# Self attention in a perceiver block: 128-wide weight transposes, values by head parity, weighing over four quarters of the array

## The chip, the cores and the metric

One NeuronCore of a Trainium2 chip runs the whole kernel. The metric is the device time of one execution in microseconds, as the median of several runs. A profile of one execution comes with it: a page of summary views, and a trace of every instruction with its start, its duration and what it waited for. TensorE is called PE in these views, its weight loads PEld, VectorE DVE, ScalarE ACT, GpSimd POOL, and SyncE, which issues the DMAs, SP.

## What is computed

Sixteen sequences of 64 rows of 512 pass through three residual blocks: a cross attention to a context of 512 rows, a self attention with two softmaxes a head, and a feed-forward with 4-bit rounding of its operands. The change touches the second block and the hand-over to the third. The second, cut to what matters:

```
x = x + self_attention(layernorm(x))
q, k, v = z @ Wq.T, z @ Wk.T, z @ Wv.T        # 8 heads, in q and k two halves of 32 a head
q, k = rope(q), rope(k)
o1 = softmax(q1 @ k1.T * d**-0.25) @ v        # v: 64 wide a head
o2 = softmax(q2 @ k2.T * d**-0.25) @ v
o = o1 - lam * o2
o = o * rsqrt(mean(o*o) + eps) * ln_w + ln_b  # over a head's 64
return (o * (1 - LAMBDA_INIT)) @ Wo.T
```

The feed-forward is `silu(gate) * up`, then `down`, where each operand is rounded in blocks of 16 (a block's maximum, a scale, a rounding, the scale again).

## The kernel before

Rows are taken in eight tiles of 128, each two sequences (e = 0, 1) of 64 rows. Matmuls that need precision are split: an operand is a high part (`copy` to the rounded type on ScalarE) and a low part (the difference, on VectorE or POOL), and a product of 128x512 is twelve matmuls in three groups of four (`terms`, L114). Plain fp32 matmuls stand as two records each in the profile; transposes as one.

`cross_attention` (L346) ends with the start of the self attention: the weights Wq, Wk, Wv, Wo are loaded and split (`split`, L1146), and tiles 0 and 1 get their first products. Then `SelfAttention.rest` (L1369) runs a software pipeline over the tiles n = 2 to 7. A round n does for tile n the products Wq, Wk, Wv, rope (`rope`, L1183: VectorE multiplies by the tables at L1198 and L1200, POOL adds at L1206), the transposes of q and k (`turn_qk`, L1209: qt and kt on TensorE, copies qT and kT on ScalarE at L1216), the scores (`scores`, L1219: sc), and the softmax (`softmax`, L1236: mx at L1245 and ex at L1246 on VectorE; exp at L1255; the sum at L1260). In the same round tile n-1 gets the mix of its two softmaxes (`mix`, L1265: VectorE at L1268, POOL at L1271), the transpose of the mixed weights w (`turn_w`, L1275: wt on TensorE at L1282, the copy wT at L1290), the weighing of the values (`weigh`, L1292: o at L1298), the squares (L1308) and the norm's factor (`rms`, L1310; two POOL operations, rstd). Tile n-2 gets `scale` (L1316, VectorE), `turn_o` (L1320: ot, then oT at L1326 and a split) and `out` (L1338: the product wo and the addition of x, VectorE, L1346). Tile n+1 gets its norm z (ScalarE, L166) and its transpose zt with the split into zh and zl (`turn`, L1161). `end` (L1348) holds the order from qt to the sum.

The order of each engine is the order in which the program writes it: `in_order` (L82), called at the end of `rest`, ties every instruction so far to the one before it on its engine. The feed-forward's later steps are placed by a scheduler, which also draws some of their layer-norm statistics (st_f, mv_f) forward into the gaps of `rest`.

Into the rounds 3 to 7 are laid the norm steps of the feed-forward's tiles 0 and 1: `norm_steps` (L1492) gives seven steps a tile (statistics; normalise; then the five steps of `fp4_steps`, L180: maxima and scales at L194 to L197; POOL's multiplication L199; a VectorE operation L202 with a Relu on ScalarE L205; two VectorE operations L207 and L208; POOL's multiplication L210). `rest` says in `parts` how many steps go ahead of `out`, behind it, and behind `end`.

```python
norms = iter(first[:3] + second[:1] + first[3:4] + second[1:2] + first[4:] + second[2:])
parts = {3: (1, 0, 1), 4: (2, 1, 1), 5: (1, 1, 1), 6: (1, 1, 0), 7: (1, 1, 1)}
```

PSUM has eight banks of 128x512. Three turn round for products and transposes (`mm` and `tr`, L99 and L102: the same three), two pairs turn round for scores and gate/up products (`two`, L105), one is for weighing and for down products (`ps_av`). A tile waits for the last reader of the one whose place it takes.

After the rounds the written order goes on: the gate and up products of (tile 0, chunk 0), the rest of tiles 6 and 7, first steps of the feed-forward (`gate` L1521, `gated` L1534, `quantise`). Loads of the feed-forward's weights (`weights`, L1451) are issued from SP at fixed places of this order.

Of the kernel before, what the change touches and what calls it, by code (L numbers as in the profile page):

```python
# [9 lines left out]
F32 = mybir.dt.float32  # L10
# [3 lines left out]
AF = mybir.ActivationFunctionType  # L14
ALU = mybir.AluOpType
# [4 lines left out]
P = 128  # L20
D = 512
KC = D // P
B = 16
S = 64
N = 512
NJ = N // P
NT = B * S // P
FF = 1408
BLK = 16
CHUNKS = [(at, min(D, FF - at)) for at in range(0, FF, D)]  # L30
# [15 lines left out]
def f32(t):  # L46

    return t.bitcast(F32)


class Common:
# [75 lines left out]
    def split(self, hi, lo, src, by=None):  # L127

        self.nc.scalar.copy(hi, src)  # L129
        (by or self.nc.vector).tensor_tensor(lo, src, f32(hi), ALU.subtract)  # L130
# [165 lines left out]
class Context:  # L296
# [59 lines left out]
    def high(self, b, c):  # L356
        if b < B:
            if c == 0:
                self.done[b] = tuple(
                    self.cm.slot(6 + 2 * (b % 2) + h, f"x{h}_{b}") for h in range(2)  # L360
                )
            self.cm.nc.scalar.copy(self.done[b][0][:, c, :], self.raw[:, c, :])  # L362

    def low(self, b, c):
        if b < B:
            hi, lo = (t[:, c, :] for t in self.done[b])
            by = (self.cm.nc.vector, self.cm.nc.gpsimd)[c % 2]
            by.tensor_tensor(lo, self.raw[:, c, :], f32(hi), ALU.subtract)  # L368
# [360 lines left out]
def cross_attention(tc, cm, sc, i, cw, cx, w1, w2, att, quant):  # L729

    nc = tc.nc
# [9 lines left out]
    for e in range(2):  # L741
        t = w2.tile([P, S + N + S + KC * S], F32, tag=f"fx{e}", name=f"mask{e}")
# [202 lines left out]
    def out_product(p):  # L945
        oh, ol = state.pop(("oT", p))
        po = cm.mm(f"po_{p}")
        cm.product(
            po, lambda k: (oh[:, k, :], ol[:, k, :], w_o[0][:, k, :], w_o[1][:, k, :]), range(KC)
        )  # L950
        state["po", p] = po, cm.moments(po, f"o_{p}")

    def out_norm(p):
        po, mv = state.pop(("po", p))
        z = w2.tile([P, D], F32, tag="one", name=f"oz_{p}")
        cm.normalize(z, po, f"o_{p}", mv)
        state["oz", p] = z

    def out_add(p):
        z = state.pop(("oz", p))  # L960
        nc.gpsimd.tensor_tensor(z, z, rows_o["g_o"], ALU.mult)
        nc.gpsimd.tensor_tensor(z, z, rows_o["b_o"], ALU.add)
        nc.gpsimd.tensor_tensor(cm.x[p], cm.x[p], z, ALU.add)

    def out_moments(p):
        cm.shift(cm.x[p], f"a_{p}", cm.x_mv[:, p, :])
# [140 lines left out]
    att.values(0)  # L1107
    out_moments(NT - 2)
    att.end(0, sum=False)
    att.split("Wo", 0, 1)  # L1110
    att.sum(0)
    att.product(1, "Wq")
    att.mix(0)
# [4 lines left out]
    att.rope(1, "Wk")  # L1118
    att.norm(2)
    out_product(NT - 1)  # L1120
    att.split("Wo", 2, 3)
    out_norm(NT - 1)
    att.end(1)
    assert not quant.active and not quant.jobs
    return {2: lambda: out_add(NT - 1), 3: lambda: out_moments(NT - 1)}


class SelfAttention:
# [15 lines left out]
        self.nc.sync.dma_start(raw, self.i[name].rearrange("(k p) n -> p k n", p=P))  # L1144

    def split(self, name, *ks):  # L1146
        cm, raw = self.cm, self.st[name, "raw"]
        if ks[0] == 0:
            at = self.HOME[name]
            self.W[name] = cm.slot(at, f"{name}h"), cm.slot(at + 1, f"{name}l")  # L1150
        hi, lo = self.W[name]
        for k in ks:
            cm.split(hi[:, k, :], lo[:, k, :], raw[:, k, :], (self.nc.vector, self.nc.gpsimd)[k % 2])

    def norm(self, t):
        cm = self.cm
# [20 lines left out]
        self.st["ps", t, name] = ps  # L1177

    def values(self, t):
        v = self.st["v", t] = self.w1.tile([P, D], F32, tag="v", bufs=4, name=f"v_{t}")  # L1180
        self.nc.scalar.copy(v, self.st.pop(("ps", t, "Wv")))

    def rope(self, t, name):  # L1183
        nc, w1, sa = self.nc, self.w1, self.sa
# [90 lines left out]
    def turn_w(self, t):  # L1275
        cm, nc = self.cm, self.nc
        w = self.st.pop(("w", t))
        pt = cm.tr(f"wt_{t}").rearrange("p (h n) -> p h n", n=S)
        for h in range(8):
            for e in range(2):  # L1280
                rows = slice(e * S, (e + 1) * S)
                nc.tensor.matmul(  # L1282
                    pt[rows, h, :],
                    lhsT=w[rows, h, :],
                    rhs=cm.ident[rows, rows],
                    start=True,
                    stop=True,
                )
        wT = self.st["wT", t] = self.w2.tile([P, 8, S], F32, tag="four0", name=f"wT_{t}")
        nc.scalar.copy(wT, pt)  # L1290

    def weigh(self, t):  # L1292
        v, wT = self.st.pop(("v", t)), self.st.pop(("wT", t))
        po = self.st["po", t] = self.cm.ps_av.tile([P, 8, S], F32, tag="av", name=f"o_{t}")
        for h in range(8):
            for e in range(2):
                rows = slice(e * S, (e + 1) * S)
                self.nc.tensor.matmul(  # L1298
                    po[rows, h, :],
                    lhsT=wT[rows, h, :],  # L1300
                    rhs=v[rows, h * S : (h + 1) * S],
                    start=True,
                    stop=True,
                )

    def squares(self, t):
        o = self.st["o", t] = self.w1.tile([P, 8, S], F32, tag="oh", name=f"on_{t}")
        self.nc.scalar.activation(o, self.st["po", t], AF.Square)  # L1308

    def rms(self, t):  # L1310
        cm = self.cm
# [3 lines left out]

    def scale(self, t):  # L1316
        r = self.st.pop(("r", t)).unsqueeze(2).to_broadcast([P, 8, S])
        self.nc.vector.tensor_tensor(self.st["o", t], self.st.pop(("po", t)), r, ALU.mult)

    def turn_o(self, t):  # L1320
        cm, nc, sa = self.cm, self.nc, self.sa
# [16 lines left out]
    def out(self, t):  # L1338
        cm = self.cm
        oh, ol = self.st.pop(("oT", t))  # L1340
        ps = cm.mm(f"wo_{t}")
        wh, wl = self.W["Wo"]
        cm.product(
            ps, lambda k: (oh[:, k, :], ol[:, k, :], wh[:, k, :], wl[:, k, :]), range(KC)
        )
        self.nc.vector.tensor_tensor(cm.x[t], ps, cm.x[t], ALU.add)  # L1346
# [22 lines left out]
    def rest(self, ff, last):  # L1369

        first, second = (ff.norm_steps(t) for t in range(2))
        norms = iter(first[:3] + second[:1] + first[3:4] + second[1:2] + first[4:] + second[2:])


        parts = {3: (1, 0, 1), 4: (2, 1, 1), 5: (1, 1, 1), 6: (1, 1, 0), 7: (1, 1, 1)}

        def steps(n, part):  # L1380
            for _ in range(parts[n][part] if n in parts else 0):
                next(norms)()

        for n in range(2, NT):
            self.product(n, "Wq")
            self.scale(n - 2)
            self.product(n, "Wk")
            if n == NT - 1:
                ff.weights(("g", 1))
            self.mix(n - 1)  # L1390
            self.turn_o(n - 2)
            self.rope(n, "Wq")
            self.product(n, "Wv")
            if n == NT - 1:
                ff.weights(("u", 1), ("d", 0))
            self.values(n)
            if n + 1 < NT:
                self.norm(n + 1)
            self.rope(n, "Wk")
            steps(n, 0)  # L1400
            if n == NT - 1:
                ff.turn(0)
            self.out(n - 2)
            last.get(n, lambda: None)()
            if n == 2:
                ff.weights(("g", 0), ("u", 0))
            steps(n, 1)
            self.end(n)
            steps(n, 2)
        assert not list(norms)  # L1410
        ff.gate((0, 0))
        self.scale(NT - 2)
        self.mix(NT - 1)
        ff.up((0, 0))
        self.turn_o(NT - 2)
        ff.gated((0, 0))
        ff.turn(1)
        ff.gate((0, 1))
        self.turn_w(NT - 1)
        ff.quantise((0, 0))  # L1420
        ff.weights(("d", 1))
        ff.gate((1, 0))
        self.weigh(NT - 1)
        self.squares(NT - 1)
        self.rms(NT - 1)
        self.out(NT - 2)
        ff.weights(("g", 2))
        ff.up((0, 1))
        self.scale(NT - 1)
        ff.hidden((0, 1))  # L1430
        self.turn_o(NT - 1)
        ff.up((1, 0))
        ff.hidden((1, 0))
        ff.turn_h((0, 0))
        self.out(NT - 1)
        ff.weights(("u", 2), ("d", 2))
        self.cm.in_order()


class FeedForward:  # L1440
# [65 lines left out]

    def turn(self, t):
        cm, w2 = self.cm, self.w2
        pt = cm.tr(f"xt_{t}")
        cm.transpose_chunks(pt, self.st.pop(("z", t)), KC)  # L1510
        both = w2.tile([P, 2, KC, P], F32R, tag=f"fx{t % 2}", name=f"fx_{t}")
        cm.split(both[:, 0], both[:, 1], pt.rearrange("p (k n) -> p k n", n=P))
        self.st["x", t] = both[:, 0], both[:, 1]
# [6 lines left out]

    def gate(self, s):  # L1521
        t, c = s
        both = self.cm.two(f"gu_{t}_{c}")
        self.st["gu", s] = [both[:, w, : CHUNKS[c][1]] for w in range(2)]
        self.half(s, "g", self.st["gu", s][0])

    def up(self, s):
# [177 lines left out]
```

## Time and profile before

| | |
|---|---|
| median of 3 runs | 918.56 us (917.95 to 920.64) |
| the profiled execution | 917.56 us, span 915.8 us |
| TensorE's granted clock | 0.999 of full speed |
| TensorE busy, 600 to 617 us and 652 to 669 us | 16.42 and 16.67 of 17 us |
| VectorE busy, the same stretches | 12.19 and 12.53 us |
| TensorE busy, 750 to 916 us | 161.30 of 166 us |

The busy shares of the stages come from the view of engine time by stretch. In a line of the timeline the columns are: start and duration in us, engine, line of the kernel, operation, the tile written and the tiles read, partitions and elements, count, and in brackets the engine's idle time ahead of it with what ended it. A line of the waits gives the waiting engine and line, what it waited for, the sum in us, how often, and the longest.

### The profile page before, as it was taken

To read this page: it belongs to the slowest core of one execution; us is meant where nothing else is said; L and a number is where in the kernel's file an instruction comes from. 1 tells how busy PE (TensorE), PEld (TensorE's weight loads), DVE (VectorE), ACT (ScalarE), POOL (GpSimd) and SP (SyncE) were. 2 spreads that over 40 slices of the span, in tenths; PEclk is the share of its full clock that TensorE was granted. 3 is DMA by queue.
4 is the path that set the end of the run, shared out by engine and by line. 5 is a ranking of instruction groups with operands and counts; after the bars stand their busy time and mean duration, and the time that the engine had idled before them with its cause. 6 is when DMAs were issued, how large, how long until landed. Compare 5 with 4: busy or idle time off the path is not lost.

```text
span 915.8 us, 17531 instructions
## 1 busy us (share of the span) xinstructions
PE 896.2 (98%) x6774; PEld 741.3 (81%) x6774; DVE 687.8 (75%) x1386; ACT 392.7 (43%) x750; POOL 330.0 (36%) x376
## 2 busy tenths in 40 slices
PE   5999999999999999999999999999999999999998
PEld 5898777878887788787878887878778788888886
DVE  6544467788799787786987864576887698888875
ACT  4464444444454434444544455434444333322221
POOL 5245153335253353252533522565564320100000
PEclk9999999999999999999999999999999999999999
DMA  7464565544465445445644351140005530000000
GB/s 246 169 242 138 160 185 159 175 157 145 152 184 155 140 143 166 128 131 143 198 135 149 104 168 70 48 184 3 1 1 232 207 138 12 13 12 12 13 12 23
DMA packets 80234, 111.11 MB, mean 121 GB/s; under 512 B 33160, under 2 KB 38808, under 8 KB 78872
## 3 DMA queue, kind: packets, MB, share of 16 engines
q1 hardware_dynamic: 79992, 109.48, 37.2%
q8 instruction: 53, 0.87, 0.4%
q0 software_dynamic: 160, 0.52, 0.2%
q14 instruction: 29, 0.24, 0.1%
HBM read 84.26 MB, written 25.72 MB: 120 GB/s over the span
## 4 chain that ended last, share of the span: by engine, by line
PE 86%; DVE 6%; DMA 2%; ACT 2%; POOL 1%; SPq 1%; issue 1%; ACTq 0%; DVEq 0%; POOLq 0%
PE pk L121 19%; PE pv L121 18%; PE gu L121 13%; PE dn L121 7%; PE av L904 4%; PE sim L836 4%; PE prt L171 3%; PE lv L121 2%; PE po L121 2%; PE lq L121 2%; PE lk L121 2%; PE wo L121 2%; PE Wv L121 2%; PE ht L171 1%; DMA raw_wo<-in_w_out_dram 1%; PE Wq L121 1%
## 5 line engine op out<-in xcount | busy, mean ns | idle before, releaser
L121 PE MATMUL pv<-xvh,x 128*128 128x512 f32 x512 | 133.1, 392 | 0.0
L121 PE MATMUL pk<-x,xkh 128*128 128x512 f32 x512 | 130.4, 397 | 0.0
L121 PEld LDWEIGHTS pk<-x,xkh 128*128 128x128 f32 x512 | 93.7, 188 | 25.4 <-issue 3.9
L121 PEld LDWEIGHTS pv<-xvh,x 128*128 128x128 f32 x512 | 95.3, 188 | 23.3 <-issue 2.2
L810 DVE TENSOR_TENSOR k<-pk,row 128x512 f32<-128x512 f32 x64 | 43.7, 684 | 47.4 <-PE pk L121 47.4
L823 ACT ACTIVATE v<-pv,rs 128x512 f32<-128x512 f32 x64 | 43.9, 686 | 79.2 <-PE pv L121 79.1
L859 ACT ACTIVATE pr<-pr,least 128x576 f32<-128x576 f32 x64 | 49.2, 772 | 55.3 <-DVE least L855 55.0
L368 POOL TENSOR_TENSOR x<-raw,x 128x512 fp32r<-128x512 f32 x32 | 44.2, 1382 | 77.8 <-ACT x L362 71.5
L121 PE MATMUL pk<-x,xkl 128*128 128x512 f32 x256 | 68.6, 390 | 0.0
L121 PE MATMUL pv<-xvl,x 128*128 128x512 f32 x256 | 68.5, 389 | 0.0
L121 PE MATMUL gu<-uT,fx 128*128 128x512 f32 (+1 forms) x288 | 67.3, 377 | 0.0
L121 PE MATMUL gu<-gT,fx 128*128 128x512 f32 (+1 forms) x288 | 65.5, 375 | 1.1 <-DVE h L1541 0.6
L121 PEld LDWEIGHTS gu<-gT,fx 128*128 128x128 f32 x288 | 52.2, 188 | 9.0 <-ACT fx L129 0.9
L121 PEld LDWEIGHTS gu<-uT,fx 128*128 128x128 f32 x288 | 51.9, 188 | 7.2
L121 PEld LDWEIGHTS pk<-x,xkl 128*128 128x128 f32 x256 | 48.1, 188 | 10.3
L121 PEld LDWEIGHTS pv<-xvl,x 128*128 128x128 f32 x256 | 48.1, 188 | 10.2
L855 DVE CUSTOM_DVE_ANT_0 pr<-sim,mask 128x576 f32<-128x576 f32 x64 | 45.9, 755 | 6.3 <-PE sim L836 5.6
L121 PE MATMUL dn<-dT,hh 128*128 128x512 f32 x176 | 44.8, 394 | 0.6 <-ACT hh L129 0.6
L321 DVE BATCH_NORM_STATS2 cst<-nat 128x6 f32<-128x512 f32 x64 | 42.8, 669 | 3.4 <-DMA nat<-in_ctx_dram 3.4
L205 ACT ACTIVATE qe_h<-qe_h,mmagic 128x512 f32<-128x512 f32 (+1 forms) x24 | 16.5, 689 | 67.2 <-DVE qe_h L202 64.1
L871 ACT COPY prT<-prt 128x512 f32<-128x512 f32 x64 | 34.1, 585 | 18.1 <-PE prt L171 18.1
L904 PEld LDWEIGHTS av<-v,prT 128*64 128x64 f32 x1024 | 36.7, 138 | 5.6 <-issue 5.6
(302 smaller groups left out, 1976.5 us busy)
## 6 DMA issues: line engine op xcount, KB each, us to landing
nat<-in_ctx_dram SPq DMA_DIRECT2D x16, 1024.0 KB
raw<-in_ctxT_dram SPq DMA_DIRECT2D x64, 256.0 KB
d_d<-qhl_d SPq DMA_DIRECT2D x11, 512.0 KB
row<-rs_d SPq DMA_DIRECT2D x16, 256.0 KB
g_d<-qhl_g SPq DMA_DIRECT2D x8, 512.0 KB
u_d<-qhl_u SPq DMA_DIRECT2D x8, 512.0 KB
gT<-g_d SPq DMA_DIRECT2D x4, 1024.0 KB
uT<-u_d SPq DMA_DIRECT2D x4, 1024.0 KB
```

The lines of the kernel that those rows point to most:

```text
L121: self.nc.tensor.matmul(ps, lhsT=p[i], rhs=p[j], start=start and n == 0, stop=stop and n == last)
L171: self.nc.tensor.transpose(pt[:, c * P : (c + 1) * P], src[:, c * P : (c + 1) * P], self.ident)
L205: nc.scalar.activation(e, e, AF.Relu, bias=self.mmagic, scale=MAGIC)
L321: nc.vector.bn_stats(st, self.nat[b][:, j, :])
L368: by.tensor_tensor(lo, self.raw[:, c, :], f32(hi), ALU.subtract)
L810: nc.vector.tensor_tensor(k[:, S : S + N], ps, cx.row[b], ALU.mult)
L823: nc.scalar.mul(v, ps, cx.rs[b][:, t : t + 1])
L836: nc.tensor.matmul(pss[r][c * S : (c + 1) * S, h, :half], lhsT=queries[b % 2][rows, m, :], rhs=st["k"][m][rows, at : at + half], start=Tru ...
L855: nc.vector.tensor_tensor_reduce(two(pr), ps[:, :, :half], two(mask), -1.0, BIG, ALU.add, ALU.min, least)
L859: nc.scalar.activation(pr, pr, AF.Exp, bias=least, scale=-1.0, accum_out=st["tot"][:, t : t + 1])
L871: nc.scalar.copy(prT, pt.rearrange("p (j q) -> p j q", q=P))
L904: nc.tensor.matmul(st["av"][rows, 2 * a + r, :], lhsT=w[:, rows], rhs=v[:, at : at + S], start=(n == 0), stop=(n == len(pairs) - 1),)
```

## The change

It consists of these edits, all in the self attention, its entry and its exit:

- `turn_w` turns w in four full 128x128 transposes in place of sixteen 64x64 matmuls against the identity; a transposed square then holds two heads, one above the other, in its partitions.
- `values` copies v in four pieces of 64 partitions x 256, so that even heads lie in partitions 0 to 63 and odd ones in 64 to 127, for each sequence.
- `weigh` runs its sixteen 64x64 matmuls over all four combinations of row half (head parity) and column half (sequence); even heads are written to one bank (av), odd ones to another (of the three). `squares` and `scale` become two instructions each.
- `out` uses a pair of the score banks for tiles 0 to 5; the feed-forward's second transpose uses the bank av; the first gate and up products use two of the three banks.
- Two norm steps change their places, and `parts` changes.
- Wo's four high parts are copied together, its low parts are made later.
- `gated((0, 0))` goes ahead of `turn_o(NT - 2)`.

```diff
-    att.split("Wo", 0, 1)
+    att.high("Wo", *range(KC))
     att.sum(0)
...
     out_product(NT - 1)
-    att.split("Wo", 2, 3)
+    att.low("Wo", 0, 1)
     out_norm(NT - 1)
+    att.low("Wo", 2, 3)
     att.end(1)
...
     def values(self, t):
-        v = self.st["v", t] = self.w1.tile([P, D], F32, tag="v", bufs=4, name=f"v_{t}")
-        self.nc.scalar.copy(v, self.st.pop(("ps", t, "Wv")))
+        v = self.st["v", t] = self.w1.tile([P, 2, KC, S], F32, tag="v", bufs=4, name=f"v_{t}")
+        ps = self.st.pop(("ps", t, "Wv")).rearrange("p (c h d) -> p c h d", h=2, d=S)
+        for e in range(2):
+            for h in range(2):
+                self.nc.scalar.copy(v[h * S : (h + 1) * S, e], ps[e * S : (e + 1) * S, :, h, :])
...
     def turn_w(self, t):
-        pt = cm.tr(f"wt_{t}").rearrange("p (h n) -> p h n", n=S)
-        for h in range(8):
-            for e in range(2):
-                rows = slice(e * S, (e + 1) * S)
-                nc.tensor.matmul(
-                    pt[rows, h, :],
-                    lhsT=w[rows, h, :],
-                    rhs=cm.ident[rows, rows],
-                    start=True,
-                    stop=True,
-                )
+        pt = cm.tr(f"wt_{t}")
+        cm.transpose_chunks(pt, w.rearrange("p h t -> p (h t)"), KC)
...
     def weigh(self, t):
-        po = self.st["po", t] = self.cm.ps_av.tile([P, 8, S], F32, tag="av", name=f"o_{t}")
-        for h in range(8):
-            for e in range(2):
-                rows = slice(e * S, (e + 1) * S)
-                self.nc.tensor.matmul(
-                    po[rows, h, :],
-                    lhsT=wT[rows, h, :],
-                    rhs=v[rows, h * S : (h + 1) * S],
+        even = self.cm.ps_av.tile([P, D], F32, tag="av", name=f"o_{t}_0")
+        po = self.st["po", t] = [
+            ps[:, : KC * S].rearrange("p (c d) -> p c d", d=S)
+            for ps in (even, self.cm.tr(f"o_{t}_1"))
+        ]
+        for c in range(KC):
+            for h in range(2):
+                rows = slice(h * S, (h + 1) * S)
+                for e in range(2):
+                    cols = slice(e * S, (e + 1) * S)
+                    self.nc.tensor.matmul(
+                        po[h][cols, c, :],
+                        lhsT=wT[rows, c, cols],
+                        rhs=v[rows, e, c, :],
...
     def squares(self, t):
-        self.nc.scalar.activation(o, self.st["po", t], AF.Square)
+        for h, po in enumerate(self.st["po", t]):
+            self.nc.scalar.activation(by_half(o)[:, h], po, AF.Square)
...
     def scale(self, t):
-        self.nc.vector.tensor_tensor(self.st["o", t], self.st.pop(("po", t)), r, ALU.mult)
+        for h, po in enumerate(self.st.pop(("po", t))):
+            self.nc.vector.tensor_tensor(
+                by_half(self.st["o", t])[:, h], po, by_half(r)[:, h], ALU.mult
+            )
...
     def out(self, t):
-        ps = cm.mm(f"wo_{t}")
+        ps = cm.two(f"wo_{t}")[:, 0, :] if t < NT - 2 else cm.mm(f"wo_{t}")
...
-        norms = iter(first[:3] + second[:1] + first[3:4] + second[1:2] + first[4:] + second[2:])
-        parts = {3: (1, 0, 1), 4: (2, 1, 1), 5: (1, 1, 1), 6: (1, 1, 0), 7: (1, 1, 1)}
+        norms = iter(first[:2] + second[:1] + first[2:4] + second[1:2] + first[4:] + second[2:])
+        parts = {3: (1, 0, 1), 4: (1, 2, 1), 5: (1, 2, 0), 6: (0, 2, 0), 7: (1, 2, 0)}
...
         ff.up((0, 0))
+        ff.gated((0, 0))
         self.turn_o(NT - 2)
-        ff.gated((0, 0))
...
     def turn(self, t):
-        pt = cm.tr(f"xt_{t}")
+        pt = cm.ps_av.tile([P, D], F32, tag="av", name="xt_1") if t == 1 else cm.tr(f"xt_{t}")
...
     def gate(self, s):
-        both = self.cm.two(f"gu_{t}_{c}")
-        self.st["gu", s] = [both[:, w, : CHUNKS[c][1]] for w in range(2)]
+        if s == (0, 0):
+            both = [self.cm.mm(f"gu_{w}") for w in range(2)]
+        else:
+            pair = self.cm.two(f"gu_{t}_{c}")
+            both = [pair[:, w, :] for w in range(2)]
+        self.st["gu", s] = [ps[:, : CHUNKS[c][1]] for ps in both]
```

The lines move a little: the addition of x is L1368 after the change, `scale` L1338, `weigh` L1316, the value copies L1201, kT's copy L1236.

More of the change, by code (lines that the diff above doesn't have):

```diff
@@ L1125, in cross_attention, with by_half @@
     return {2: lambda: out_add(NT - 1), 3: lambda: out_moments(NT - 1)}
+def by_half(t):
+    return t.rearrange("p (c h) d -> p h c d", h=2)
 class SelfAttention:
@@ L1146, in split, with high, low @@
     def split(self, name, *ks):
-        cm, raw = self.cm, self.st[name, "raw"]
+        for k in ks:
+            self.high(name, k)
+            self.low(name, k)
+    def high(self, name, *ks):
         if ks[0] == 0:
             at = self.HOME[name]
-            self.W[name] = cm.slot(at, f"{name}h"), cm.slot(at + 1, f"{name}l")
+            self.W[name] = self.cm.slot(at, f"{name}h"), self.cm.slot(at + 1, f"{name}l")
+        for k in ks:
+            self.nc.scalar.copy(self.W[name][0][:, k, :], self.st[name, "raw"][:, k, :])
+    def low(self, name, *ks):
         hi, lo = self.W[name]
         for k in ks:
-            cm.split(hi[:, k, :], lo[:, k, :], raw[:, k, :], (self.nc.vector, self.nc.gpsimd)[k % 2])
+            (self.nc.vector, self.nc.gpsimd)[k % 2].tensor_tensor(
+                lo[:, k, :], self.st[name, "raw"][:, k, :], f32(hi[:, k, :]), ALU.subtract
+            )
     def norm(self, t):
@@ L1277, in turn_w @@
         w = self.st.pop(("w", t))
-        pt = cm.tr(f"wt_{t}").rearrange("p (h n) -> p h n", n=S)
-        for h in range(8):
-            for e in range(2):
-                rows = slice(e * S, (e + 1) * S)
-                nc.tensor.matmul(
-                    pt[rows, h, :],
-                    lhsT=w[rows, h, :],
-                    rhs=cm.ident[rows, rows],
-                    start=True,
-                    stop=True,
-                )
-        wT = self.st["wT", t] = self.w2.tile([P, 8, S], F32, tag="four0", name=f"wT_{t}")
@@ L1290, in turn_w @@
-        nc.scalar.copy(wT, pt)
+        pt = cm.tr(f"wt_{t}")
+        cm.transpose_chunks(pt, w.rearrange("p h t -> p (h t)"), KC)
+        wT = self.st["wT", t] = self.w2.tile([P, KC, P], F32, tag="four0", name=f"wT_{t}")
+        nc.scalar.copy(wT, pt.rearrange("p (c n) -> p c n", n=P))
     def weigh(self, t):
         v, wT = self.st.pop(("v", t)), self.st.pop(("wT", t))
-        po = self.st["po", t] = self.cm.ps_av.tile([P, 8, S], F32, tag="av", name=f"o_{t}")
-        for h in range(8):
-            for e in range(2):
-                rows = slice(e * S, (e + 1) * S)
-                self.nc.tensor.matmul(
-                    po[rows, h, :],
-                    lhsT=wT[rows, h, :],
-                    rhs=v[rows, h * S : (h + 1) * S],
-                    start=True,
-                    stop=True,
-                )
+        even = self.cm.ps_av.tile([P, D], F32, tag="av", name=f"o_{t}_0")
@@ new lines, in weigh @@
+        po = self.st["po", t] = [
[11 more added lines that the diff above has]
+                        rhs=v[rows, e, c, :],
+                        start=True,
+                        stop=True,
+                    )
@@ L1317, in scale @@
         r = self.st.pop(("r", t)).unsqueeze(2).to_broadcast([P, 8, S])
-        self.nc.vector.tensor_tensor(self.st["o", t], self.st.pop(("po", t)), r, ALU.mult)
+        for h, po in enumerate(self.st.pop(("po", t))):
+            self.nc.vector.tensor_tensor(
+                by_half(self.st["o", t])[:, h], po, by_half(r)[:, h], ALU.mult
+            )
     def turn_o(self, t):
```

## The prediction

> **What bounds the kernel now.** I read the page first. TensorE is busy for 98% of the span at full clock, so whatever it loses or gains is likely to be time. The change touches only the self-attention stage (about 584 to 735 us) and the first steps of the feed-forward.
>
> ```profile
> span 915.8 us, 17531 instructions
> PE 896.2 (98%) x6774; PEld 741.3 (81%) x6774; DVE 687.8 (75%) x1386; ACT 392.7 (43%) x750; POOL 330.0 (36%) x376
> ```
>
> Busy shares do not tell whether TensorE's work or a chain through the others sets the pace, so I took the timeline of one round of the loop in `rest` (n = 3), TensorE's first, then ScalarE's, VectorE's and two lines of the others. I count from the start of kt, TensorE's transpose of the keys. It starts at 617.88 and, one round later, at 634.24: a period of 16.36 us.
>
> ```profile
> 617.88 0.60 PE L171 MATMUL kt<-ident,rc_k 128*128 128x128 f32 x4
> 618.41 1.15 PE L1282 MATMUL wt<-ident,w 64*64 64x64 f32 x32
> 619.49 0.66 PE L171 MATMUL zt<-ident,z 128*128 128x128 f32 x4
> 620.08 0.91 PE L1228 MATMUL sc<-kT,qT 32*64 32x64 f32 x64
> 620.92 1.15 PE L1298 MATMUL o<-v,wT 64*64 64x64 f32 x32
> ```
> ```profile
> 618.56 0.59 ACT L1216 COPY kT<-kt 128x512 f32<-128x512 f32 x1
> 619.61 0.59 ACT L1290 COPY wT<-wt 128x512 f32<-128x512 f32 x1 [0.46 <-PE wt L1282]
> 620.18 0.59 ACT L129 CAST zh<-zt 128x512 fp32r<-128x512 f32 x1
> ```
> ```profile
> 620.80 0.69 DVE L130 TENSOR_TENSOR zl<-zt,zh 128x512 fp32r<-128x512 f32 x1 [2.47 <-ACT zh L129]
> 621.41 0.68 DVE L1245 TENSOR_REDUCE mx<-sc 128x8 f32<-128x512 f32 x1
> ...
> 627.08 0.68 DVE L1318 TENSOR_TENSOR on<-o,rstd_o 128x512 f32<-128x512 f32 x1
> ```
> ```profile
> 627.82 0.42 PEld L171 LDWEIGHTS ot<-ident,on 128*128 128x128 f32 x4 [0.47 <-DVE on L1318]
> ...
> 632.82 1.29 POOL L1206 TENSOR_TENSOR rc_k<-rc_k,rs_k 128x512 f32<-128x512 f32 x1
> ```
>
> The reader should see two loops of nearly the same length. TensorE has no real gap. But ot already waits for VectorE's `scale` (L1318), and POOL's last rope sum ends at 634.1, just before kt needs it. So there is a chain: kt, the ScalarE copies up to zh, zl, softmax, exp, sum, scale, mix, four POOL operations, kt. It has some 0.1 us of slack, which decides what TensorE's savings are worth.
>
> Last I read the waits and the neighbours of long VectorE operations in the rounds with feed-forward norm steps (n = 4 to 7), whose periods are 17.6, 17.1 and 17.2 us.
>
> ```profile
> PE wt L1282 <- DVE x L1346: 1.4, 2, 1.1
> ```
> ```profile
> 649.17 1.28 POOL L1206 TENSOR_TENSOR rc_k<-rc_k,rs_k 128x512 f32<-128x512 f32 x1
> 649.28 1.21 DVE L196 TENSOR_SCALAR qm_x<-qs_x 128x32 f32<-128x32 f32 x1
> ...
> 677.17 1.06 POOL L210 TENSOR_TENSOR fz<-fz,qs_x 128x512 f32<-128x512 f32 x1
> 677.32 0.94 DVE L1263 TENSOR_SCALAR sm<-sm,neglam 128x8 f32<-128x8 f32 x1
> ```
>
> A tiny VectorE tensor_scalar, 0.2 us elsewhere, ends only with POOL's operation beside it. In rounds 4 and 6 this holds up x's addition (L1346), whose bank wt needs; in round 5 and at the end it delays scale.
>
> **The change part by part.**
>
> *Transposes of w.* Sixteen 64x64 matmuls take 1.08 us from wt to the next start; four 128x128 transposes take 0.44 (qt to kt). TensorE saves 0.64 a tile, 5.1 over eight.
>
> *Weighing in quarters.* The same 16 matmuls (32 records) take 1.08 us now, with row and column halves equal, so two quarters of the array work. sc shows the near row: 64 records over four row groups in 0.84 us, 13 ns each against 34. With four quarters I take 0.5 us (15.6 ns each), saving 0.58 a tile, 4.6 in all. Bounds: no saving (a bank for each row half buys nothing) and 0.66 (sc's pace). The Trainium skill, "TensorEngine Tiling (Array Packing)", PSUM Bottleneck, speaks against counting this: tiling speeds up TensorE but not the evacuation of PSUM, and the copy may become the bottleneck. By TensorE's rows alone the two edits make a round 16.36 - 1.22 = 15.1. By the rule the copies behind them decide. Here the rule is nearer, as the ot wait shows, so I work the chain.
>
> *The chain of a light round after the change.* kT's copy starts at kt + 0.68 as before. wT follows it directly at + 1.2 (its data are there at + 1.0), zh at + 1.75, zl at + 2.4, mx at + 3.0; before, mx was at + 3.53. sc waits for kT and ends near + 2.3, so it is not later than zl. From mx to scale's end nothing changes (6.3 us) but that scale is now two 128x256 operations; the rs pair of that shape spans 0.66 against 0.60, so + 0.06. Two squares instead of one lie before exp, which waits for VectorE anyway (1.59 us idle). Then mix and POOL as before. The period becomes 16.36 - 0.53 + 0.06 = 15.9. TensorE, with 15.1 of work, now waits some 0.8 a round, mostly at ot: most of its saving is not paid out, and the weighing's speed is free in the rounds.
>
> *wo in a score bank, norm steps moved.* wt no longer waits for L1346; the second score tile does, but sc comes 1.4 us after kt and the addition ends near kt + 0.2. The first quantising step now stands behind the addition, when rc_k is over: 0.7 + 0.2 + 0.2 + 0.35 with hoisted statistics (0.86) between, against 3.1 contended. Together they end near kt + 2.6, so zl is 0.2 late in rounds 4 and 6. Uncovered, at its contended 3.1, zl would be 1.8 late. In round 5, L210 moves ahead of the round's end and scale's 0.71 wait goes. Six loops (kt from 601.56 to 702.51, 100.95 us) become 6 x 15.9 + 0.6 = 96.0: 4.95 saved.
>
> *Values as four 64x256 copies.* Nearest row: 128x256 at 0.37 to 0.39. Following copies start about 0.1 before the last ends, so 0.28 each, 1.12 in all against 0.48. In the rounds they start 3.1 before kt, and with z (0.72) and, in 5 and 7, a Relu (0.62) still end before qT is wanted: hidden, with 0.4 to 1 us to spare. At tile 0 nothing covers them: sc already waits 0.32 for kT. Cost 0.64. Bounds 0.5 and 1.9 (each as dear as 128x512).
>
> *Wo's four high copies at once, low parts later.* sum(0) no longer sits behind L130, which waited for ScalarE: VectorE's chain is 1.1 earlier, and kt's wait for rc_k at tile 1 (0.58, with its latency 0.77) goes. Low parts move to where VectorE idles (0.46 + 0.72 + 0.95); POOL's two take 2.6 us before rstd is wanted 3 us later. Start: + 0.64 - 0.77 = -0.13.
>
> *First feed-forward steps.* From kt(7) to tile 7's ot takes 24.75 us. Removed: two wt (1.28), two weighings (1.16), gate's wait for a score bank (0.52; it now takes two product banks, free once kT and wT are copied) and the 0.60 for h, which sat behind oT, fz, oh and a table load on ScalarE and now goes ahead of them. That is 3.56. Given back: sc waits 0.45 for kT, as no zt lies between; ot of tile 6 comes 0.8 to 1.3 before scale is done (fx and x's addition sit in front of mx, pushed by the value copies), of which I take 0.8. That leaves 2.3. The weights' transfers are issued in the same order and each use moves less than its issue; the last pair (issued after wo of tile 7, at 739.78) keeps its distance to its use. Beyond, TensorE runs nearly without gaps and VectorE moves with it.
>
> Sum: 0.13 + 4.95 + 2.3 = 7.4. The profiled execution took 917.56 (span 915.8), so 910.2. The median of the runs, 918.56, lies 1.0 above it: 911.2.
>
> **The rivals.**
>
> *TensorE stays the bound.* If the chain has more slack than I read, all of 5.1 + 4.6 and the stalls (0.58, 1.39, 0.79, 0.52, 0.60) come out, less 0.64 at tile 0: some 13, or 905.6. For it: the gapless timeline. Against: ot waits for scale already.
>
> *The moved steps only move the wait.* If the quantising step costs 3.1 behind the addition too (POOL runs statistics there), zl is 1.8 late in two rounds: 7.4 - 3.2 = 4.2 saved, 914.4.
>
> *The value copies take over, slower than before.* Place: ScalarE's queue between Wv's end and qT, 3.2 us long. With z it is full at (3.2 - 0.72) / 4 = 0.62 us a copy; beyond, each further 0.1 costs 0.4 in each of six rounds and at tile 0. The gain is eaten at about 0.8. At 1.0 us (halves of the partitions crossing, each dearer than a full copy) it is 6 x 1.52 + 3.5 - 8.0 = 4.6 worse: 923. Against it: no PSUM copy of this size is above 0.4.
>
> *It doesn't do what it says.* If quarters do not run four abreast, only the end pays: 1.16 less, 912.4.
>
> **How the numbers follow.** Chain bound 0.63 (911.2), TensorE bound 0.17 (905.6), moved wait 0.13 (914.4), no packing 0.03, value copies 0.04 (923). A measurement of this kernel can tell about 0.3%, 2.8 us, from no change, so faster means below 915.8. All but the last case and a third of the moved wait's lie there: faster 0.92, same 0.04, slower 0.04. 0.3 us on each of six periods is 1.8, and the end is uncertain by 1: the likeliest case spans 908.5 to 914. To reach the neighbours on both sides I give 905.5 to 915.
>
> **What would show it.** Right: wt at 0.44 and o near 0.5 us; periods of kt near 15.9; TensorE's waits at ot for L1338 of 0.5 to 1 us a round; no wait for L1368; qs and qm at 0.2; a longer kT wait at tile 0. Wrong: periods at 15.1 without waits (TensorE bound), zl late by more than 1 us in rounds 4 and 6, or qT starting well after qt's end. What would make the forecast wrong as a whole is a copy above 0.6 us, or a feed-forward stage that gives the gain back.

## The result, and the profile after

The median went from 918.25 us (917.83 to 920.64, 4 runs) to 912.52 us (912.35 to 913.16, 4 runs): ratio 0.9937, 95% interval 0.9925 to 0.9949. The gain is 5.73 us; 7.4 was forecast. The profiled execution took 912.59 us.

The page's head: TensorE has 9.3 us less work than before (896.2), and the span is 5.1 us shorter.

```profile
span 910.7 us, 17129 instructions
...
PE 886.9 (97%) x6550; PEld 733.2 (81%) x6550; DVE 682.1 (75%) x1394; ACT 399.9 (44%) x782; POOL 330.5 (36%) x376
```

From here on a round n is the stretch from tile n's kt to tile n+1's kt; what it shows of ot belongs to tile n-1. TensorE's timeline of the round n = 3 (the prediction's lines are of the stretch before it, from tile 2's kt on):

```profile
635.70 0.60 PE L171 MATMUL kt<-ident,rc_k 128*128 128x128 f32 x4
636.13 0.60 PE L171 MATMUL wt<-ident,w 128*128 128x128 f32 x4
636.57 0.62 PE L171 MATMUL zt<-ident,z 128*128 128x128 f32 x4
637.13 0.91 PE L1248 MATMUL sc<-kT,qT 32*64 32x64 f32 x64
637.97 0.69 PE L1316 MATMUL o<-v,wT 64*64 64x64 f32 x32
638.59 1.20 PE L121 MATMUL Wq<-Wqh,zh 128*128 128x512 f32 x4
...
645.06 0.65 PE L171 MATMUL ot<-ident,on 128*128 128x128 f32 x4 [0.73 <-DVE on L1338]
```

From wt to the next start are 0.44 us, from o to the next 0.62 (before: 1.08 each). Both edits do what they say, and ot now waits 0.73 us for the scaling (L1338). The chain of waits that ended last, followed back over this round, says through what (pieces under 0.05 us are left out):

```profile
636.48 0.49 ACT kT L1236
636.97 0.28 ACT wT L1301
637.25 0.08 issue
637.33 0.63 ACT zh L129
637.98 0.69 DVE zl L130
638.67 0.61 DVE mx L1265
639.38 0.69 DVE ex L1266
640.07 0.61 DVE mx L1265
640.70 0.70 DVE ex L1266
641.48 1.07 ACT ex L1275
642.57 1.23 DVE sm L1280
643.83 0.26 DVE sm L1281
644.15 0.11 issue
644.25 0.76 DVE on L1338 x2
```

From kT to the scaling no piece is TensorE's: a faster weighing changes nothing here. What the rounds gained came in through the transposes: wt ends sooner, so wT, zh and zl follow sooner (mx at kt + 2.89, + 3.53 before). This is read from the traces; no run has the transposes or the weighing alone. TensorE's waits from 580 to 750 us, all of them:

```profile
PE ot L171 <- DVE on L1338: 6.1, 7, 1.5
PE zt L171 <- ACT v L1201: 0.8, 1, 0.8
PE sc L1248 <- ACT kT L1236: 0.4, 1, 0.4
PE wt L171 <- DVE fx L130: 0.3, 1, 0.3
PE wt L171 <- ACT qT L1236: 0.3, 1, 0.3
```

The wait for x's addition (1.4 us before) is gone; 6.1 us now stand at ot (0.8 before). Below, the starts of kt and of tile 7's ot are read from the same timeline of each kernel; a column is the time from one kt to the next, the last but one from the last kt to tile 7's ot.

| | kt 0 to 1 | 1 to 2 | 2 to 3 | 3 to 4 | 4 to 5 | 5 to 6 | 6 to 7 | to ot | sum |
|---|---|---|---|---|---|---|---|---|---|
| before | 14.50 | 16.32 | 16.36 | 16.33 | 17.63 | 17.13 | 17.18 | 24.75 | 140.20 |
| after | 14.77 | 17.09 | 15.76 | 15.75 | 15.88 | 15.80 | 16.25 | 22.88 | 134.18 |
| e8, order alone | 14.50 | 16.34 | 16.36 | 16.37 | 16.45 | 16.41 | 16.87 | 23.51 | 136.81 |
| e11, order undone | 14.78 | 17.09 | 15.81 | 15.78 | 17.11 | 16.47 | 17.00 | 22.67 | 136.71 |
| e12, zl behind ms | 14.79 | 16.50 | 15.22 | 15.22 | 15.33 | 15.29 | 15.72 | 22.88 | 130.95 |
| e9, three edits | 14.54 | 15.82 | 15.25 | 15.26 | 15.34 | 15.29 | 15.72 | 22.17 | 129.39 |

The stage is 6.02 us shorter. Behind it nothing is given back: tile 7's ot comes 5.0 us earlier in the span, and the span ends 5.1 us earlier. (The stage itself began 1.0 us later in this execution, at 588.08 for 587.06; in the other kept traces it begins anywhere between 587.3 and 588.8.)

### The profile page after: what moved, and what is told of

It reads as the page before. It is cut to its first block, busy times and chain, and to the rows that moved or that the text cites. A ratio compares the mean times of both kernels' runs of the same rounds, so it can differ in the third digit from the quotient of the medians.

```text
span 910.7 us, 17129 instructions
## 1 busy us (share of the span) xinstructions
PE 886.9 (97%) x6550; PEld 733.2 (81%) x6550; DVE 682.1 (75%) x1394; ACT 399.9 (44%) x782; POOL 330.5 (36%) x376
## 4 chain that ended last, share of the span: by engine, by line
PE 85%; DVE 7%; ACT 3%; DMA 2%; issue 1%; SPq 1%; POOL 1%; ACTq 0%; DVEq 0%; POOLq 0%
PE pk L121 18%; PE pv L121 18%; PE gu L121 13%; PE dn L121 7%; PE av L904 4%; PE sim L836 4%; PE prt L171 3%; PE po L121 3%; PE Wv L121 2%; PE lv L121 2%; PE wo L121 2%; PE lq L121 2%; PE lk L121 2%; DVE ex L1266 1%; PE ht L171 1%; DMA raw_wo<-in_w_out_dram 1%
```

## The experiments

Each is the changed kernel with one edit, unless it says otherwise. The kernel before ran on the same chip in each group: 918.28 us (first group: after_again, e1, e2, e3), 918.42 (second: e4, e5, e7, e10), 917.83 (third: e8, e9, e11, e12). Ratios are to it. A difference to the changed kernel is one of gains: the changed kernel's is 5.86 us (after_again), a run's is taken from the kernel before of its own group. A ratio's interval is some 1.2 us wide to each side, so a difference of 1 us or less is not clear of noise by the medians; there the columns of kt carry the reading.

**The changed kernel again.**

> The changed kernel once more, as the standard for its neighbours: 912.5 us, within 0.5.

912.42 us (911.56 to 912.8), ratio 0.9931 [0.9919, 0.9944].

**Is TensorE the bound between kt and ot?** The weighing is done twice over, with the same numbers.

```diff
-        for c in range(KC):
+        for c in 2 * list(range(KC)):
             for h in range(2):
```

> Every weighing's sixteen matmuls are issued twice (the second pass overwrites the first with the same numbers): 0.62 us more TensorE work for each of eight tiles. Chain theory: the round's wait at ot (0.71 to 0.74 us) swallows it in tiles 0 to 5, and the wait of 1.01 at tile 6; only tile 7 pays, so +0.6 us, and the ot waits shrink to about 0.1. TensorE theory (its work sets the pace): 8 x 0.62 = +5.0.

914.22 us (912.31 to 915.24), ratio 0.9948 [0.9936, 0.9961]: +1.8 by the medians. The extra work is less than was expected, since the longer burst runs faster, 1.09 us to the next start in place of 0.62:

```profile
638.67 1.16 PE L1316 MATMUL o<-v,wT 64*64 64x64 f32 x64
639.76 1.21 PE L121 MATMUL Wq<-Wqh,zh 128*128 128x512 f32 x4
```

That is 0.47 us a tile, 3.8 us in all, which is what the TensorE theory then asks for. Four of the six rounds of the profiled execution have 15.76 to 15.80 us, or 17.05 for the first, as without the extra work. Two are longer, 16.57 and 17.65, for a reason that neither theory had:

```profile
PE o L1316 <- issue: 2.6, 2, 1.6
PE ot L171 <- DVE on L1338: 1.8, 4, 1.0
```

Twice TensorE stopped inside the doubled burst, 2.6 us together, with nothing in the trace to wait for. Where it did not, the 0.47 us was taken out of ot's wait (0.23 in place of 0.74). TensorE as the bound falls for the stretch from kt to ot. What stops a burst of that length is open; the profiled execution is the slowest of the five runs, and the fastest (912.31) is no slower than the changed kernel, so the stops may not come every time.

**Shorten the chain.** If ot waits for zl, softmax, exp, sum and scale, taking zl (0.68 us) out must show. First zl went between the two halves of the softmax.

```diff
-        cm.split(zh, zl, pt.rearrange("p (k n) -> p k n", n=P))
+        src = pt.rearrange("p (k n) -> p k n", n=P)
+        self.nc.scalar.copy(zh, src)
+        self.st["zlow"] = zl, src, zh
...
+    def turn_low(self):
...
+            self.nc.vector.tensor_tensor(zl, src, f32(zh), ALU.subtract)
...
+            if n == 0:
+                self.turn_low()
```

> The low part zl of the next tile is made on VectorE after the first max/subtract pair of the softmax and not before it; no work is added or removed. Chain theory: mx starts when the scores are done (kt + 2.35) and not behind zl (kt + 2.9), so each of the six rounds is 0.55 us shorter until TensorE's 15.1 us of work bind: -3 us (-2 to -3.5), and the waits at ot fall to 0.2. TensorE theory: no change, 0, or slightly slower.

912.85 us (912.51 to 912.93), ratio 0.9937 [0.9924, 0.9949]: no gain. The expectation was at fault: exp needs both halves of the softmax, so zl still stood ahead of it (mx 637.70, zl 639.11, exp 641.21 us). Next zl of tiles 2 to 7 went behind both halves, with q's and k's products ordered so that their terms with zl come last (no run has that order alone).

```diff
         if n < NT:
             self.softmax(n)
+            self.turn_low()
             self.exp(n)
...
-            self.product(n, "Wq")
-            self.scale(n - 2)
-            self.product(n, "Wk")
+            q, k = self.terms(n, "Wq"), self.terms(n, "Wk")
+            for part in (q, q, k, k, q, k):
+                next(part)
+            self.scale(n - 2)
```

> The run before moved zl only between the two halves of the softmax, where it still lies ahead of exp; so it never left the chain. Here zl of tiles 2 to 7 is made behind the last subtraction, in VectorE's idle time beside exp, and TensorE does the groups of Wq and Wk that need zl last, so that nothing waits for it. Same instructions in all. Chain theory: exp starts 0.6 us earlier in each of six rounds, the periods of kt fall from 15.8 to 15.2 (TensorE's work is 15.1), the ot waits to 0.2: -3 us (-2 to -3.5). If something else sets the period: 0.

911.33 us (910.8 to 914.71), ratio 0.9929 [0.9916, 0.9941]: 1.2 below the changed kernel by the medians, 1.0 from the first kt to tile 7's ot, 0.15 us in most rounds. A second branch had become the last: the squares' sum ms, POOL's rstd, scale; and zl stood ahead of ms on VectorE. POOL's rstd ends at 644.12 (642.46 + 1.66), and so starts the scaling:

```profile
644.14 0.76 DVE L1356 TENSOR_TENSOR on<-o,rstd_o 128x256 f32<-128x256 f32 x2 [0.28 <-POOL rstd_o L137]
```

So zl went behind ms as well.

```diff
             self.exp(n)
         if 0 <= n - 1:
             self.rms(n - 1)
+        self.turn_low()
```

> The changed kernel with zl (the low part of the turned input) taken behind the two halves of the softmax and behind the sum of squares ms, and q's and k's products begun with the terms that need no zl. With zl ahead of ms the period fell only from 15.8 to 15.65 us, since ms, and with it rstd on POOL and the scaling that ot waits for, then came last. Theory (ot is bound by the chain softmax, exp, sum and by the chain ms, rstd, scale, whichever is later, and zl's 0.68 us stands in both): both chains are freed of zl, so the period falls by 0.4 to 0.6 us in six rounds, together 1.5 to 3 us less than the changed kernel, about 910.0. Rival (a third wait, for example q and k waiting for zl, is already as late): no better than with zl ahead of ms, 911.3, that is 1 us below the changed kernel.

908.78 us (908.14 to 909.25), ratio 0.9901 [0.9887, 0.9914]: 3.2 below the changed kernel, by the medians and in the table, a little more than expected. VectorE's timeline of the round n = 3:

```profile
638.95 0.69 DVE L1284 TENSOR_TENSOR ex<-sc,mx 128x512 f32<-128x512 f32 x1
639.56 0.68 DVE L1350 TENSOR_REDUCE ms<-on 128x8 f32<-128x512 f32 x1
640.15 0.68 DVE L1193 TENSOR_TENSOR zl<-zt,zh 128x512 fp32r<-128x512 f32 x1
640.83 1.22 DVE L1298 TENSOR_REDUCE sm<-ex 128x16 f32<-128x1024 f32 x1
642.08 0.25 DVE L1299 RECIPROCAL sm<-sm 128x16 f32<-128x16 f32 x1
642.37 0.23 DVE L1301 TENSOR_SCALAR sm<-sm,neglam 128x8 f32<-128x8 f32 x1
642.51 0.75 DVE L1356 TENSOR_TENSOR on<-o,rstd_o 128x256 f32<-128x256 f32 x2
```

zl runs while ScalarE does exp, where VectorE idled 0.59 us before. The wait of ot falls to 0.16 us and the period to 15.22, close to the 15.1 of TensorE's own work that the prediction had added up. The chain is shown as what holds ot up, from two sides: where TensorE did not stop, work added to it between kt and ot was free, and work taken from the chain was time.

From the scaling back to kt there are two ways of nearly one length: TensorE's own (ot, Wv, wo, qt), 6.39 us in the round n = 3, and the mix with the four POOL operations, whose last sum is done 0.12 us before the next kt (651.33 and 651.45). So TensorE's work behind ot does lie in the loop; no run made that part longer or shorter.

**Norm steps and wo's bank.** First the norm steps alone as before (`norms` and `parts`), then the bank alone, then both.

```diff
-        norms = iter(first[:2] + second[:1] + first[2:4] + second[1:2] + first[4:] + second[2:])
-        parts = {3: (1, 0, 1), 4: (1, 2, 1), 5: (1, 2, 0), 6: (0, 2, 0), 7: (1, 2, 0)}
+        norms = iter(first[:3] + second[:1] + first[3:4] + second[1:2] + first[4:] + second[2:])
+        parts = {3: (1, 0, 1), 4: (2, 1, 1), 5: (1, 1, 1), 6: (1, 1, 0), 7: (1, 1, 1)}
```

> Only the places of the feed-forward's norm steps are taken back to those of the kernel before. If the overlap with POOL is what they cost: the scale and maximum steps take 3.1 us again beside POOL's rope sums, the addition of x comes 1.3 us later, the second score tile waits 0.4 us in rounds 4 and 6, and scale waits 0.7 us beside L210 in round 6 and at the end: +2.0 (1.4 to 3). If the moved bank of wo alone had freed the rounds: 0.

913.32 us (913.07 to 914.89), ratio 0.9949 [0.9936, 0.9963]: +0.9 by the medians, under the expected 1.4 to 3. The five runs lie at 913.1 to 913.3 and at 914.5 to 914.9, and the profiled one, from the first kt to tile 7's ot, is 1.6 longer (135.77 for 134.18), so the price is not known better than 0.9 to 1.6. Nearly all of it is in one round (16.46 for 15.80) and the end (23.58 for 22.88). There ot waits 1.42 and 1.71 us (0.71 and 1.01 in the changed kernel), and a small VectorE operation ahead of the scaling is as long as POOL's beside it:

```profile
675.00 1.06 POOL L210 TENSOR_TENSOR fz<-fz,qs_x 128x512 f32<-128x512 f32 x1
675.15 0.94 DVE L1283 TENSOR_SCALAR sm<-sm,neglam 128x8 f32<-128x8 f32 x1
```

The overlap in the rounds 4 and 6 is back too (qs and qm take 0.84 and 1.2 us), but costs only 0.17 and 0.04 us there.

```diff
-        ps = cm.two(f"wo_{t}")[:, 0, :] if t < NT - 2 else cm.mm(f"wo_{t}")
+        ps = cm.mm(f"wo_{t}")
```

> Only wo of tiles 0 to 5 goes back to one of the three product banks, the norm steps stay moved. Theory: the addition of x no longer has norm steps ahead of it and is done at kt + 0.2, wt wants the bank at kt + 0.44: 0 (-0.2 to +0.5). Rival, the bank is the cause of what rounds 4 to 6 gained: wt waits again, 0.3 to 1.1 us in three rounds, +2.

912.03 us (911.72 to 912.33), ratio 0.9931 [0.9919, 0.9942]: -0.5 by the medians, -0.2 from the first kt to tile 7's ot, no loss.

> The changed kernel with both the places of the norm steps and the bank of wo as in the kernel before. Undone alone, the norm steps cost 0.9 us and the bank nothing (-0.4). Theory (one cover, two means: with the bank as before x's addition has to clear VectorE before wt's bank is free, and norm steps ahead of it hold it up, so each edit alone covers most of it): undone together 2 to 4 us, periods of rounds 4 to 6 at 16.2 us or more in place of 15.8. Rival (the two are independent): the sum of the single runs, about +0.5 us.

914.52 us (914.2 to 914.88), ratio 0.9963 [0.9951, 0.9976]: +2.5, by the medians and in the table, inside the expected 2 to 4 and well above the sum of the two (0.4 by the medians, 1.4 from kt to ot). All of it is in the columns from kt 4 to kt 7. TensorE's waits have the old one back:

```profile
PE ot L171 <- DVE on L1338: 6.5, 7, 1.5
PE wt L171 <- DVE x L1368: 1.4, 2, 1.1
```

With the old bank and a norm step ahead of x's addition, wt waits for that addition. The runs with one of the two undone have no such wait at all, so each edit alone covers it, and its price (1.12 and 0.31 us, in the rounds 4 and 6) can be read only from the run with both undone. The 0.7 us of POOL's L210 beside the sum is another matter: only the place of the norm steps takes it away.

Now the same from the other side: the kernel before, with only the order and the banks of the change (norm steps, wo's bank, the first gate pair's banks and place, the second turned input's bank).

> The kernel before with the edits of order and banks alone (norm steps, wo's bank, the first feed-forward pair in other banks and issued earlier, the second turned input in another bank), and none of the edits to weights, values, weighing or Wo. Theory (the norm steps and wo's bank take rounds 4 to 6 from 17.6, 17.1 and 17.2 us to the 16.35 us of the earlier rounds, 2.9 us, and the end gives 0.8): 3.5 us less than the kernel before, range 2.5 to 4, leaving about 2.2 us for the packing of the weighing. Rival (the packed weighing brings nearly all and the order only matters once TensorE is shorter): under 1 us.

914.65 us (913.72 to 915.35), ratio 0.9965 [0.9953, 0.9978]: 3.2 below the kernel before, 3.39 in the table, as expected. The rounds 4 to 6 fall to 16.4 to 16.9, the first three keep 16.35. TensorE's waits from 580 to 750 us are two:

```profile
PE kt L171 <- POOL rc_k L1206: 0.6, 1, 0.6
PE sc L1228 <- ACT kT L1216: 0.3, 1, 0.3
```

So over half of the gain needs no packing. Packing on top of it, with the value copies and Wo's new places that came with it, brings 136.81 - 134.18 = 2.63 us of the 9 that TensorE saves: some 0.6 in each of the last six columns, less 1.0 in the first two.

**The start: two edits.** Wo's low parts 0 and 2 go ahead of tile 7's cross attention output and norm:

```diff
+    att.low("Wo", 0, 2)
     att.norm(2)
     out_product(NT - 1)
-    att.low("Wo", 0, 1)
     out_norm(NT - 1)
-    att.low("Wo", 2, 3)
+    att.low("Wo", 1, 3)
```

> Wo's two low parts on VectorE are made right behind rope of tile 1, where VectorE idles 1.6 us, and POOL's two behind out_norm; in the changed kernel they lie between po's statistics and zl of tile 2, where one takes 1.03 us beside POOL's. Theory: zl of tile 2 comes 0.9 us earlier and the period from tile 1 to 2 falls from 17.1 to 16.2: -0.9 us (-0.5 to -1). If the long period has another cause: 0.

911.82 us (911.13 to 912.55), ratio 0.9928 [0.9916, 0.994]: -0.7. The first round of the loop falls from 17.09 to 16.41, as expected.

Half of tile 0's value copies on VectorE:

```diff
+                if t == 0 and e:
+                    self.nc.vector.tensor_copy(dst, src)
+                else:
+                    self.nc.scalar.copy(dst, src)
```

> Of tile 0's four value copies VectorE makes two. Theory: the copies take 0.75 us in place of 1.5, zt's bank and kT come that much earlier, TensorE has no other wait before tile 1: -0.75 us (-0.4 to -0.9). If the wait at tile 0 were covered later: 0.

911.32 us (910.56 to 911.53), ratio 0.9921 [0.9909, 0.9934]: -1.2, more than the expected 0.4 to 0.9. The first column falls from 14.77 to 14.11, which was expected. The rest is at the end (22.17 for 22.88), where the edit itself changes nothing: tile 6's ot waits 0.23 us in place of 1.01, since a drawn-forward norm (fz, 0.82 us on ScalarE) stands behind the split of fx and not ahead of it.

**All three.** zl behind ms, the shared copies, the earlier low parts:

> The changed kernel with three edits together: zl behind ms, half of the value copies of the first tile on VectorE, and two of the four low parts of Wo ahead of tile 2. The last two alone gave 1.1 and 0.6 us. If the three add up: 3 to 4.5 us less than the changed kernel, about 908.5. If the gain of the last two is swallowed by another wait at the start: 1.5 to 2.5 us less, about 910.5.

907.07 us (906.98 to 907.46), ratio 0.9884 [0.9869, 0.9899]: 4.9 below the changed kernel by the medians (4.8 in the table), a little more than the 3 to 4.5 expected, and 10.8 below the kernel before. Of this, 0.7 is at the end, as in the run before.

## Why the prediction was right, and where its sum was off

**The mechanism held.** What ot waits for is the chain that it named, the period of light rounds is 15.76 (15.9 forecast), the wait stands at ot with 0.71 to 0.74 us in the rounds from 2 on, and most of what TensorE saves is not paid out. One piece differs: it closed the loop over the mix and POOL, and the chain in the trace goes from ot to kt over TensorE. The two ways end 0.12 us apart, so the period is the same. The rule that it drew on (the Trainium skill, "TensorEngine Tiling (Array Packing)", PSUM Bottleneck: tiling does not speed up what empties PSUM) came nearer than TensorE's own rows: 15.8 and not 15.1. It held in direction only: of the chain's pieces, just the scaling reads what the packed weighing wrote. e12 shows that the 15.1 is there to be had once the chain is shorter.

**Weighing.** 0.62 us and not 0.5: 19 ns a record where 15.6 was taken. In the rounds this cost nothing, being beside the chain.

**The six loops.** 96.53 us against 96.0. Rounds 2 to 6 together took 79.44 us, 0.66 below their forecast of 80.1; zl of rounds 4 and 6 was not 0.2 late, and only round 6 (16.25, with the feed-forward's first transpose in it) lies above 15.9. The mis-sized term is the first loop, 17.09 where 15.9 was taken. "Low parts move to where VectorE idles" looked at what the low parts would delay on POOL, and not at what stands behind them on VectorE:

```profile
604.84 0.81 DVE L155 TENSOR_SCALAR oz<-po,mv_o 128x512 f32<-128x512 f32 x1 [0.72 <-POOL mv_o L149]
605.56 1.03 DVE L1167 TENSOR_TENSOR Wol<-Wor,Woh 128x512 fp32r<-128x512 f32 x1
606.52 0.68 DVE L130 TENSOR_TENSOR zl<-zt,zh 128x512 fp32r<-128x512 f32 x1
```

zl starts 3.67 us after kt (602.85), not 2.4, and ot of that round waits 1.47. e4 returned 0.7 of it. There zl still starts 2.99 after kt, right behind oz, the cross attention's last norm, which waits for POOL: the rest of the first loop's excess is not the low parts'.

**The start.** +0.27 us and not -0.13. The step that failed is "start about 0.1 before the last ends, so 0.28 each". ScalarE's timeline:

```profile
587.90 1.50 ACT L1201 COPY v<-Wv 64x256 f32<-64x256 f32 x4 [1.36 <-PE Wv L121]
589.42 0.58 ACT L1236 COPY qT<-qt 128x512 f32<-128x512 f32 x1
```

Four take 1.50, 0.375 each: they do not overlap. And zt, which the prediction did not name, takes the bank that they read (its 0.8 us wait stands in the list of waits above). sc comes 1.04 us later after kt than before, where 0.64 was taken. The bounds given (0.5 to 1.9) held both, 1.50 and 1.04. In the rounds the copies are hidden, as forecast.

**Norm steps and bank.** Right in sign and sum, but not two gains that add up: in the rounds 4 and 6 each covers the same wait. In round 5 the scaling's wait beside L210 went, as forecast, by the norm steps alone. x's addition ends 0.46 us after kt and not 0.2 (651.22 + 0.69, kt 651.45), which cost nothing. qs and qm fell to 0.16 us as forecast:

```profile
653.02 0.16 DVE L195 TENSOR_SCALAR qs_x<-qm_x 128x32 f32<-128x32 f32 x1
653.23 0.16 DVE L196 TENSOR_SCALAR qm_x<-qs_x 128x32 f32<-128x32 f32 x1
```

**The end.** 1.87 us and not 2.3. The mis-sized term is how late the scaling is for ot of tile 6: ot waits 1.01 us for it where 0.8 was taken. From kt to this ot are 9.70 us, and the forecast's terms give 9.68 - 0.64 - 0.58 - 0.52 + 0.45 + 0.8 = 9.19. (The 0.45, sc's wait for kT, does not come; wt waits 0.30 for fx in its place, which was not counted.) From there to tile 7's ot it is 13.18, 0.07 better than forecast. The scaling is late because of fx's split, which stands behind the value copies, a norm and a Relu on ScalarE; with the norm behind the split (e5) ot waits only 0.23, and wt not at all for fx.

The rivals: TensorE as the bound (905.6) falls by the waits at ot and by e1. That the moved steps only move their wait (914.4) falls by the 15.88 and 16.25 us of the rounds 4 and 6, where it asked for some 1.6 more each. The value copies stayed at 0.375 us, far below the 0.8 at which the gain is eaten. That packing does nothing falls by wt and o. By the table the sum is 6.02 against 7.4: 1.19 is lost in the first loop, 0.40 at the start and 0.43 at the end, and the later rounds return 0.66. Little of the agreement is luck, since only this last term offsets the others.

## What to carry to other kernels

When two loops of nearly the same length run side by side, cost a saving on one of them by the slack to the other, then ask what small thing can leave the second loop: here 0.68 us of VectorE work, moved to where the engine idles, brought more (3.2 us in the table) than the packing did on top of the order (2.6, with what its entry cost). Ask also on which part of a loop added work lies: doubling the weighing tests TensorE only between kt and ot. Move such work behind every branch that meets at the next wait, since moving it past one branch only (e10) brought a third of it. When two edits may cover one wait, undo both together before calling either worthless.

## What the runs showed of the hardware

- ScalarE copies of 64x256 from PSUM took 0.375 us each in a row without overlap, as much as a single 128x256 (0.37 to 0.39 before); two squares of 128x256 took 0.66 together.
- With 64 records of scores and 32 of weighing in a row TensorE had no pause in any round; with 64 of weighing it stopped in two of them in the one execution traced, for 0.95 and 1.64 us, with no releaser in the trace. The line is the end of such a burst:

```profile
656.57 0.33 PE L1316 MATMUL o<-v,wT 64*64 64x64 f32 x3 [0.95 <-issue]
```

- A VectorE operation of 128x8 took 0.94 us beside POOL's 128x512 multiplication and 0.23 elsewhere; in e3 that made ot's wait 0.7 us longer, twice.
- 64x64 weighing matmuls over four quarters of the array ran at 19 ns a record (0.62 us for 32) and at 17 in a burst of 64 (1.09 us), the 32x64 scores over four row groups at 13 ns (0.84 us for 64).
